# Turning score maxima into rows on VectorE in place of TensorE, in a fused AdaLN block

## The chip, the core and the metric

The kernel runs on one core of one Trainium2 chip. The metric is the device time of one execution in microseconds (us), as a median over several executions. A core has five engines, each with an instruction queue of its own: TensorE (PE, matrix products and transposes, results in PSUM), VectorE (DVE), ScalarE (ACT), GpSimd (POOL) and SyncE (SP, which here only issues DMA transfers).

## The reference, cut to what matters

The reference is one transformer block with adaptive layer norm over x of 4 batches, 1024 tokens and 256 features. Attention has 16 heads of 16 features. Behind it stands a feed-forward stage that chooses one of 8 adapters for each batch.

```python
mod = (silu(c) @ wmod).reshape(4, 6, 1, 256)   # sa, ca, ga, sb, cb, gb; ga and gb kept off zero
h = layernorm(x) * (1 + ca) + sa
q, k, v = split(h @ qkv_w.T)                   # 16 heads of 16
probs = softmax(q @ k.T / 4)                   # 1024 x 1024 per head and batch
x = x + ga * ((probs @ v) @ proj_w.T + proj_b)
h = layernorm(x) * (1 + cb) + sb
# 8 encoder/decoder pairs reconstruct h; the one of least error picks the adapter
x = x + gb * (h @ W_base + b_base + relu(h @ W_down[a] + b_down[a]) @ W_up[a] + b_up[a])
```

The softmax needs the greatest score of each query before it takes exponentials, so that these stay in range.

## The kernel before, in words

**Groups and halves.** Attention is worked in 16 groups: 4 batches times 4 groups of 4 heads. Within a group, the 1024 queries are cut into two halves of 512, and a half into 4 tiles of 128.

**First pass, the maxima (row_max).** For each pair of heads, each query tile and each half of the keys, two matmuls at L607 write scores (ps, 128 queries x 2 heads x 512 keys) to a PSUM buffer of the tag "big". VectorE takes their greatest value along the keys, negated, into mx (L614). A half of a group needs 16 such reductions. Behind the last of them VectorE takes the minimum over the two key halves (L617) and writes it into mpad, a padded 128 x 128 tile. What results has queries along partitions.

**From columns to rows (to_row).** The second pass wants the maxima as rows, queries along the free dimension. One step after the minimum, the transpose is put at the head of a list called urgent. The planner takes it in the middle of the next pair of steps, in place of another dense item. PE turns mpad into pmx (L567), a buffer of the tag "msc", of which there is one; VectorE copies 32 rows of it to SBUF (mfull, L569); GpSimd (for the very first half, where `alone` still holds, VectorE) splits each value into a high part of the shortened type float32r and the rest (mrow, L572 and L573). One step later SP stores the rows of the half to a DRAM scratch tensor (mdram, L576), and one step later again it reads them back into 2 x 4 rows of mt (L587), in the arrangement that the second pass wants. For the very first group (`soon`) store and reading are issued at once.

**Second pass (step_of).** `begin` computes the scores again, turned (pt, keys along partitions, L713): two matmuls of k and q, and two more that add the negated maxima from mt by way of the constant matrices `picks`, high part and rest together. ScalarE takes the exponential (es, L721). `weigh` multiplies es with the values (pv, L667). One step is one tile of 128 keys with one half of the queries; there are 256 steps.

**Buffers that tie the engines together.** ps, pt and the decoder's pr (L834, read by VectorE at L837 into df) share the tag "big", three buffers of two PSUM banks. A fourth such product must wait until the reader of the first, VectorE for ps and pr, ScalarE for pt, has finished.

**Order.** The order of instructions on PE and SP is written out by hand throughout. VectorE, ScalarE and GpSimd follow the hand order in the first group, and after it the order that the framework's scheduler gives. The main loop takes two steps at a time and lays them out by a pattern of letters: t for the two halves of a `begin`, S for score pairs of a later group, V for a `weigh`, R for a decoder product. At the first V it calls `dense`, which takes an item from the streams of pending work (projections, encoders, v and q/k products); `tick` counts down what `defer` has put off. The streams are served by how urgent they are.

**The start.** The first half of group 0 is computed in the opening stage, beside weight transposes and conditioning (the list `beside`). Behind its 16 score products come the transpose, the last `beside` items and two v products (pvp, L466), three more score products, and then the first step.

Of the kernel before, what the change touches and what calls it, by code (L numbers as in the profile page):

```python
# [8 lines left out]
F32 = mybir.dt.float32  # L9
F32R = mybir.dt.float32r  # L10
# [3 lines left out]
ALU = mybir.AluOpType  # L14
# [3 lines left out]
P = 128  # L18
HD = 16
HG = 4  # L20
STRIP = 32
# [5 lines left out]
def tile_adaln_block(  # L27
# [21 lines left out]
    nc = tc.nc  # L49
    B, S, D = x.shape  # L50
    NE, _, FH = w_enc.shape
    R = w_down.shape[2]
    NT = S // P
# [6 lines left out]
    NH = S // HALF  # L60
    TH = HALF // P

    cst = ctx.enter_context(tc.tile_pool(name="cst", bufs=1))
# [14 lines left out]
    st = ctx.enter_context(tc.tile_pool(name="st", bufs=3))  # L78
# [39 lines left out]
    ident = cst.tile([P, P], F32, name="ident")  # L118
# [15 lines left out]
    for n in range(2):  # L134
        t = cst.tile([P, S], F32R, name=f"mt{n}")
# [11 lines left out]
    for n in range(NV):  # L147
        t = cst.tile([P, NT, HG, STRIP], F32, name=f"vaug{n}")
# [31 lines left out]
    mdram = [dram.tile([NH, 2, HG * TH, P], F32, name=f"mdram_{n}") for n in range(2)]  # L180
# [99 lines left out]
    FULL = 0.86  # L280
# [4 lines left out]
    def defer(steps, f):  # L285
        later.append([steps, f])

    def tick():
        for entry in list(later):
            entry[0] -= 1  # L290
            if entry[0] <= 0:
                later.remove(entry)
                entry[1]()

    spare, alone, over = [0], [True], []
# [256 lines left out]


    aT_of = {}
    urgent = []

    def row_max(b, g):

        n = (b * NG + g) % 2
        mx = st.tile([P, NH, NH, HG, TH], F32, tag="mx", name=f"mx_{b}_{g}", bufs=2)  # L560


        soon = b + g == 0

        def to_row(hq):
            pm = msc_tile([P, P], f"pmx_{b}_{g}_{hq}")
            nc.tensor.transpose(pm, mpad[n], ident)  # L567
            mfull = st.tile([HG * NT, P], F32, tag="mfull", name=f"mfull_{b}_{g}", bufs=1)
            nc.vector.tensor_copy(mfull, pm[: HG * NT, :])  # L569
            mrow = st.tile([HG * NT, 2, P], F32R, tag="mrow", name=f"mrow_{b}_{g}", bufs=1)  # L570
            eng = nc.vector if alone else nc.gpsimd
            eng.tensor_copy(mrow[:, 0, :], mfull)  # L572
            eng.tensor_tensor(mrow[:, 1, :], mfull, mrow[:, 0, :].bitcast(F32), ALU.subtract)  # L573

            def store():
                nc.sync.dma_start(  # L576
                    mdram[n][hq].rearrange("l r c -> r l c"),
                    mrow[hq * HG * TH : (hq + 1) * HG * TH].bitcast(F32),
                )
                if soon:  # L580
                    back()
                else:
                    defer(1, back)

            def back():
                for a in range(2):
                    nc.sync.dma_start(  # L587
                        mt[n][a * DUO : a * DUO + HG, hq * HALF : (hq + 1) * HALF].bitcast(F32),
                        mdram[n][hq, :, a * HG * TH // 2 : (a + 1) * HG * TH // 2, :].rearrange(
                            "l (i t) c -> l i (t c)", i=HG // 2  # L590
                        ),
                    )

            if soon:
                store()
            else:
                defer(1, store)

        for half in range(NH):
            pairs = [(i, half, t, h) for h in range(NH) for i in range(2) for t in range(TH)]  # L600
            for i, hq, t, h in pairs:
                q, k = duos["q", b, g, i], duos["k", b, g, i]
                t0 = hq * HALF + t * P
                ps = big_tile([P, 2, HALF], f"ps_{b}_{g}_{hq}_{t}_{h}_{i}")
                for a in range(2):
                    r = slice(a * DUO, (a + 1) * DUO)
                    nc.tensor.matmul(  # L607
                        ps[:, a, :],
                        q[r, t0 : t0 + P],
                        k[r, h * HALF : (h + 1) * HALF],  # L610
                        start=True,
                        stop=True,
                    )
                nc.vector.tensor_reduce(mx[:, h, hq, i::2, t], ps, AX.X, ALU.max, negate=True)  # L614
                if (i, hq, t, h) == pairs[-1]:
                    rows = mpad[n][:, : HG * NT].rearrange("p (q j t) -> p q j t", q=NH, t=TH)
                    nc.vector.tensor_tensor(rows[:, half], mx[:, 0, half], mx[:, 1, half], ALU.min)  # L617
                    defer(1, lambda half=half: urgent.append(("D", 0.0, [lambda: to_row(half)])))
                yield

    def turned(b, ch, h):
# [501 lines left out]
    for i in range(2):  # L1123
        t = cst.tile([P, 1], F32, name=f"row{i}")
# [3 lines left out]
        pick = cst.tile([P, P], F32R, name=f"pick{i}")  # L1128
        nc.vector.tensor_copy(pick, t.to_broadcast([P, P]))
        picks.append(pick)  # L1130
    mpad = []
    for n in range(2):
        t = cst.tile([P, P], F32, name=f"mpad{n}")
        nc.gpsimd.memset(t, 0.0)
        mpad.append(t)
    mean_w = cst.tile([P, P], F32, name="mean_w")
    nc.gpsimd.memset(mean_w, 1.0 / (S * D))
    widened("k", 0, 0)
# [29 lines left out]
    beside += [lambda o=o: turn_weights(wqkv, qn, o, spare_tile) for o in (1, NC + 1)]  # L1168
    beside.append(lambda: turn_biases(spare_tile))
    maxima = row_max(0, 0)  # L1170
    FIRST = PAIRS // NH
    for n in range(FIRST):
# [5 lines left out]
            expand(0, 1, n - 9)  # L1178
        if n and beside:
            beside.pop(0)()  # L1180
    tick()
    all_of(Stream(list(urgent)))
    tick()
    for f in beside + v_first[1:]:
        f()
# [63 lines left out]

    alone.clear()  # L1250
    unweighed = []
    streams = [Stream(urgent)]
    streams[0].at = len(urgent)

    def ready(k, kind):

        found = []
        for s in streams:
            item = s.head(k)
            if item is not None and item[0] == kind:  # L1260
                found.append(s)
        return sorted(found, key=lambda s: (s.head(k)[-1] != "first", -s.pace(k)))

    def take(s, k):
        item = s.head(k)
# [12 lines left out]

    def dense(k, tiles, now):

        moves(k)
        if now and ready(k, "D") and streams[0].head(k) is not None:
            take(streams[0], k)[2][0]()
            return
        small = 2
        while True:
            found = [
                s
                for s in ready(k, "D")
                if s is not streams[0] and (small if s.head(k)[1] < FULL else tiles) > 0  # L1290
            ]
            if not found:
                return
            item = take(found[0], k)
            for f in item[2]:
                f()
            if item[1] < FULL:
                small, tiles = small - 1, tiles if now is False else 0
            else:
                small, tiles = 0, tiles - 1  # L1300
            moves(k)
# [7 lines left out]
    for k0 in range(0, len(order) * NT, 2):  # L1309
        b, g, h = order[k0 // NT]  # L1310
# [17 lines left out]
        tiles = sum(s.head(k0)[1] >= FULL for s in ready(k0, "D"))  # L1328
# [5 lines left out]
        k, n_t, n_s, n_v = k0, 0, 0, 0  # L1334
# [3 lines left out]
        for what in PATTERN[kind]:  # L1338
            if what == "t":
                if n_t % 2 == 0:  # L1340
                    k = k0 + n_t // 2
# [10 lines left out]
            elif what == "V":  # L1352
# [82 lines left out]
```

## Time and profile before

| | |
|---|---|
| median of 3 runs | 1140.88 us (1139.20 to 1141.67) |
| profiled execution, its own time | 1142.01 us |
| its span | 1140.2 us, 16547 instructions |
| granted TensorE clock, mean | 0.987 |
| ScalarE busy | 702.7 us (62%) |
| GpSimd busy | 263.3 us (23%) |
| mx reductions on VectorE, L614 | 512, 614.3 us, 1221 ns each |
| es exponentials on ScalarE, L721 | 512, 509.6 us, 1021 ns each |
| idle time of VectorE in front of L614 | 189.4 us, of it 184.1 us waiting for ps |

The profile page gives the busy time of each engine, then the span cut into 40 slices with the busy share in tenths, then groups of instructions by line with the mean duration. PEld is the weight load of TensorE, which overlaps its matmuls. Ends of matmuls are modelled, so a busy TensorE is not TensorE at its peak, and neighbouring matmuls can overlap in the record. A timeline row gives the start and the busy time in us, the engine, the line, the operation, the tiles it writes and reads, and how many like instructions are merged; a bracket tells of idle time in front of it and of what ended that. In front of a DMA row stands SPq, the queue that issues it, and the time is that of the issue, not of the landing.

### The profile page before, as it was taken

Reading aid. Unit: us, or ns where it says so; the run is one execution under the profiler, and the core shown is the slowest. Engines: PE = TensorE matmul, PEld = TensorE weight load, DVE = VectorE, ACT = ScalarE, POOL = GpSimd, SP = SyncE. Lnnn points to the kernel's source line nnn. Section 1 sums busy time; section 2 is a strip of 40 time slices with the busy share of each in tenths; the row PEclk is TensorE's granted clock in tenths of the full one; section 3 lists DMA queues with packets and bytes.
Section 4 is the critical chain, followed back from the end, with each engine's and each line's share of the span. In section 5 each row is a group of like instructions: output and inputs, shape, how many; then the busy total and the mean of one; then the engine's idle time right before and its main releaser. Section 6 shows DMA issues by size and latency. Waiting matters only on the chain. (4 is left out here: it accounts for less than half of the span.)

```text
span 1140.2 us, 16547 instructions
## 1 busy us (share of the span) xinstructions
PE 1081.3 (95%) x6371; PEld 482.7 (42%) x6371; DVE 803.2 (70%) x969; ACT 702.7 (62%) x953; POOL 263.3 (23%) x310
## 2 busy tenths in 40 slices
PE   8989999999999999999999999999998999899986
PEld 4433434443444444444544443333544334335333
DVE  6677876677777576777678677887688777872454
ACT  3245766666655677776455777776465777754662
POOL 2223234213343130113345000004121000241111
PEclk9899999999999999999999999999999999999998
DMA  5522423231441302122150302020230200101001
GB/s 185 103 66 89 163 81 119 76 132 58 154 136 45 120 17 90 53 95 87 48 183 6 127 13 95 16 91 19 69 130 7 85 15 9 57 23 48 10 0 49
DMA packets 57800, 84.63 MB, mean 74 GB/s; under 512 B 24941, under 2 KB 40325, under 8 KB 55929
## 3 DMA queue, kind: packets, MB, share of 16 engines
q1 hardware_dynamic: 55664, 79.90, 21.6%
q0 software_dynamic: 1088, 2.36, 0.8%
q10 hardware_dynamic: 968, 1.32, 0.3%
q8 instruction: 50, 0.82, 0.3%
q14 instruction: 30, 0.24, 0.1%
HBM read 52.15 MB, written 24.06 MB: 67 GB/s over the span
## 5 line engine op out<-in xcount | busy, mean ns | idle before, releaser
L614 DVE TENSOR_REDUCE mx<-ps 128x2 f32<-128x1024 f32 x512 | 614.3, 1221 | 189.4 <-PE ps L607 184.1
L721 ACT ACTIVATE es<-pt 128x1024 f32<-128x1024 f32 x512 | 509.6, 1021 | 248.2 <-PE pt L713 230.8
L667 PE MATMUL pv<-es,vaug 128*32 128x512 f32 x2048 | 275.1, 608 | 0.5 <-ACT ou L678 0.3
L607 PE MATMUL ps<-k,q 64*128 64x512 f32 x1024 | 237.1, 457 | 16.2 <-DVE mx L614 11.4
L713 PE MATMUL pt<-q,k 64*128 64x512 f32 x1024 | 231.3, 436 | 14.0 <-DVE mx L614 7.1
L713 PE MATMUL pt<-mt,pick 64*128 64x512 f32 x1024 | 209.0, 392 | 0.0
L607 PEld LDWEIGHTS ps<-k,q 64*128 64x128 f32 x1024 | 97.3, 184 | 222.3 <-issue 92.9
L713 PEld LDWEIGHTS pt<-q,k 64*128 64x128 f32 x1024 | 99.8, 185 | 119.8 <-DVE mx L614 87.9
L842 ACT ACTIVATE df<-df,fbias 128x512 f32<-128x512 f32 x128 | 91.1, 713 | 63.0 <-DVE df L837 63.0
L713 PEld LDWEIGHTS pt<-mt,pick 64*128 64x128 f32 x1024 | 100.3, 185 | 12.1
L837 DVE TENSOR_TENSOR df<-pr,h2T 128x1024 f32<-128x1024 f32 x64 | 77.5, 1223 | 22.3 <-PE pr L834 14.3
L667 PEld LDWEIGHTS pv<-es,vaug 128*32 128x32 f32 x2048 | 40.6, 108 | 101.8 <-issue 91.4
L834 PE MATMUL pr<-he,wdec 64*128 64x512 f32 x256 | 65.4, 605 | 3.7 <-ACT es L721 3.2
L572 POOL CAST mrow<-mfull 32x128 fp32r<-32x128 f32 x31 | 8.7, 281 | 252.3 <-DVE mfull L569 244.3
L813 PE MATMUL ph<-h2T,wenc 128*128 128x512 f32 x128 | 64.5, 628 | 0.4 <-ACT h2T L350 0.4
L319 POOL TENSOR_TENSOR rstd_n<-ve_n,neghalf 128x4 f32<-128x4 f32 x16 | 16.5, 1033 | 115.9 <-DVE ve_n L317 113.1
L955 PE MATMUL pf<-wbg,h2T 128*128 128x256 f32 x128 | 36.5, 417 | 0.0
L813 PEld LDWEIGHTS ph<-h2T,wenc 128*128 128x128 f32 x128 | 22.0, 191 | 30.0 <-issue 28.2
L466 PE MATMUL pvp<-wqkv,hT 128*128 128x256 f32 x128 | 34.5, 419 | 0.0
L774 PE MATMUL ppj<-wpg,aT 128*128 128x256 f32 x128 | 31.9, 392 | 1.9 <-ACT he L821 1.9
L975 DVE TENSOR_TENSOR x<-pf,x 128x512 f32<-128x512 f32 x16 | 10.8, 690 | 32.5 <-PE pt L713 20.5
L505 POOL COPY vaug<-vi 128x512 f32<-128x512 f32 x13 | 8.5, 655 | 108.4 <-DMA vi<-vdram 108.4
(153 smaller groups left out, 795.8 us busy)
## 6 DMA issues: line engine op xcount, KB each, us to landing
q<-qdram SPq DMA_DIRECT2D x56, 256.0 KB
k<-kdram SPq DMA_DIRECT2D x56, 256.0 KB
qdram<-qhl SPq DMA_DIRECT2D x7, 1024.0 KB
kdram<-khl SPq DMA_DIRECT2D x7, 1024.0 KB
xin<-in_L_attn_x_dram SPq DMA_DIRECT2D x16, 256.0 KB
vdram<-vo SPq DMA_DIRECT2D x16, 256.0 KB
aT<-ou SPq DMA_DIRECT2D x32, 128.0 KB
x<-in_L_attn_x_dram SPq DMA_DIRECT2D x8, 512.0 KB
```

The source lines that it names most:

```text
L466: nc.tensor.matmul(pv[:, t, :], hT[:, c, t0 : t0 + P], wqkv[:, c, 2 * D : 3 * D], start=(c == 0), stop=(c == NC - 1),)
L607: nc.tensor.matmul(ps[:, a, :], q[r, t0 : t0 + P], k[r, h * HALF : (h + 1) * HALF], start=True, stop=True,)
L614: nc.vector.tensor_reduce(mx[:, h, hq, i::2, t], ps, AX.X, ALU.max, negate=True)
L667: nc.tensor.matmul(acc[h][j * STRIP : (j + 1) * STRIP, :], va[:, kt, j, :], es[j // 2][:, j % 2, :], start=(kt == 0), stop=(kt == NT - 1),)
L713: nc.tensor.matmul(pt[:, a, :], k[r, kt * P : (kt + 1) * P] if first else picks[i][r, :], q[r, hs] if first else mt[n % 2][r, hs], start=f ...
L721: nc.scalar.activation(e, pt, AF.Exp, scale=SCALE)
L774: nc.tensor.matmul(s["po"][:, t, :], aT_of[b, t0 // HALF][:, c, t0 % HALF : t0 % HALF + P], s["wpg"][:, c, :], start=(c == 0), stop=(c == ...
L813: nc.tensor.matmul(s["ph"], wenc[:, c, 2 * pr : 2 * pr + 2, :].rearrange("p n h -> p (n h)"), s["h2T"][:, c, hs], start=(c == 0), stop=(c ...
L834: nc.tensor.matmul(two[:, i, :], wdec[r, pr, c * P : (c + 1) * P], he[r, :], start=True, stop=True)
L837: nc.vector.tensor_tensor(df, two, h2T[:, c, hs].unsqueeze(1).to_broadcast([P, 2, HALF]), ALU.subtract)
L842: nc.scalar.activation(df[:, i, :], df[:, i, :], AF.Square, bias=bdec_of(e, c), accum_out=s["acc"][:, e, c, h : h + 1],)
L955: nc.tensor.matmul(po[u][:, t, :], s["h2T"][:, c, t0 : t0 + P], s["wbg"][:, c, :], start=(c == 0), stop=False,)
```

## The change

The minimum goes to a compact tile (least, 128 x 16). VectorE splits it there into high part and rest (mhl, 128 partitions x 2 x 16), and turns it with its own transpose, which turns each block of 32 x 32 by itself: 128 x 32 becomes four stacked blocks of 32 rows x 32 queries (mrow). Four transfers, one for each block, put the pieces of 128 bytes side by side into mdram. `to_row` is called directly behind the last reduction of a half; store and reading are put off as before. The padded tiles, the transpose on PE, the copy from PSUM, the split on GpSimd, the list urgent and its place in `dense` go.

```diff
+        least = st.tile([P, HG, TH], F32, tag="least16", ...)
 ...
         def to_row(hq):
-            pm = msc_tile([P, P], f"pmx_{b}_{g}_{hq}")
-            nc.tensor.transpose(pm, mpad[n], ident)
-            mfull = st.tile([HG * NT, P], F32, tag="mfull", ...)
-            nc.vector.tensor_copy(mfull, pm[: HG * NT, :])
-            mrow = st.tile([HG * NT, 2, P], F32R, tag="mrow", ...)
-            eng = nc.vector if alone else nc.gpsimd
-            eng.tensor_copy(mrow[:, 0, :], mfull)
-            eng.tensor_tensor(mrow[:, 1, :], mfull, mrow[:, 0, :].bitcast(F32), ALU.subtract)
+            mhl = st.tile([P, 2, HG * TH], F32R, tag="mhl", ..., bufs=2)
+            nc.vector.tensor_tensor(least, mx[:, 0, hq], mx[:, 1, hq], ALU.min)
+            flat = least.rearrange("p j t -> p (j t)")
+            nc.vector.tensor_copy(mhl[:, 0, :], flat)
+            nc.vector.tensor_tensor(mhl[:, 1, :], flat, mhl[:, 0, :].bitcast(F32), ALU.subtract)
+            mrow = st.tile([P, STRIP], F32, tag="mrow", ..., bufs=2)
+            nc.vector.transpose(mrow, mhl.rearrange("p l r -> p (l r)").bitcast(F32))
             def store():
-                nc.sync.dma_start(
-                    mdram[n][hq].rearrange("l r c -> r l c"),
-                    mrow[hq * HG * TH : (hq + 1) * HG * TH].bitcast(F32),
-                )
+                to = mdram[n][hq].rearrange("l r c -> (l r) c")
+                for u in range(P // STRIP):
+                    of = slice(u * STRIP, (u + 1) * STRIP)
+                    nc.sync.dma_start(to[:, of], mrow[of, :])
 ...
                 if (i, hq, t, h) == pairs[-1]:
-                    rows = mpad[n][:, : HG * NT].rearrange("p (q j t) -> p q j t", q=NH, t=TH)
-                    nc.vector.tensor_tensor(rows[:, half], mx[:, 0, half], mx[:, 1, half], ALU.min)
-                    defer(1, lambda half=half: urgent.append(("D", 0.0, [lambda: to_row(half)])))
+                    to_row(half)
 ...
-    all_of(Stream(list(urgent)))
-    tick()
 ...
-        if now and ready(k, "D") and streams[0].head(k) is not None:
-            take(streams[0], k)[2][0]()
-            return
```

More of the change, by code (lines that the diff above doesn't have):

```diff
@@ L554, in tile_adaln_block @@
     aT_of = {}
-    urgent = []
     def row_max(b, g):
@@ L560, in row_max @@
         mx = st.tile([P, NH, NH, HG, TH], F32, tag="mx", name=f"mx_{b}_{g}", bufs=2)
+        least = st.tile([P, HG, TH], F32, tag="least16", name=f"least_{b}_{g}", bufs=2)
         soon = b + g == 0
         def to_row(hq):
-            pm = msc_tile([P, P], f"pmx_{b}_{g}_{hq}")
[L567 to L570, printed above, removed]
-            eng = nc.vector if alone else nc.gpsimd
-            eng.tensor_copy(mrow[:, 0, :], mfull)
-            eng.tensor_tensor(mrow[:, 1, :], mfull, mrow[:, 0, :].bitcast(F32), ALU.subtract)
+            mhl = st.tile([P, 2, HG * TH], F32R, tag="mhl", name=f"mhl_{b}_{g}_{hq}", bufs=2)
+            nc.vector.tensor_tensor(least, mx[:, 0, hq], mx[:, 1, hq], ALU.min)
+            flat = least.rearrange("p j t -> p (j t)")
+            nc.vector.tensor_copy(mhl[:, 0, :], flat)
+            nc.vector.tensor_tensor(mhl[:, 1, :], flat, mhl[:, 0, :].bitcast(F32), ALU.subtract)
+            mrow = st.tile([P, STRIP], F32, tag="mrow", name=f"mrow_{b}_{g}_{hq}", bufs=2)
+            nc.vector.transpose(mrow, mhl.rearrange("p l r -> p (l r)").bitcast(F32))
             def store():
-                nc.sync.dma_start(
-                    mdram[n][hq].rearrange("l r c -> r l c"),
-                    mrow[hq * HG * TH : (hq + 1) * HG * TH].bitcast(F32),
-                )
+                to = mdram[n][hq].rearrange("l r c -> (l r) c")
+                for u in range(P // STRIP):
+                    of = slice(u * STRIP, (u + 1) * STRIP)
+                    nc.sync.dma_start(to[:, of], mrow[of, :])
                 if soon:
@@ L1130, in tile_adaln_block @@
         picks.append(pick)
[L1131 to L1135, printed above, removed]
     mean_w = cst.tile([P, P], F32, name="mean_w")
@@ L1251, in tile_adaln_block @@
     unweighed = []
-    streams = [Stream(urgent)]
-    streams[0].at = len(urgent)
+    streams = []
     def ready(k, kind):
@@ L1289, in dense @@
                 for s in ready(k, "D")
-                if s is not streams[0] and (small if s.head(k)[1] < FULL else tiles) > 0
+                if (small if s.head(k)[1] < FULL else tiles) > 0
             ]
```

## The prediction

> **What bounds the kernel now.** I read the page first: the engine sums, then the slices over time.
>
> ```profile
> PE 1081.3 (95%) x6371; PEld 482.7 (42%) x6371; DVE 803.2 (70%) x969; ACT 702.7 (62%) x953; POOL 263.3 (23%) x310
> ...
> PE   8989999999999999999999999999998999899986
> ...
> DVE  6677876677777576777678677887688777872454
> ```
>
> TensorE (PE) is busy in nearly every slice; VectorE (DVE) stands at 6 to 8 tenths. The table of stages shows how little is left in the middle:
>
> ```profile
> 400.00:600.00 200.00, 198.93 (x1193) 90.56 (x1194) 144.79 (x159) 132.31 (x185) 51.62 (x58) 1.00 0.25 82
> ```
>
> In these 200 us PE rests 1.1 us, at a granted clock of 1.00. So work taken off PE shortens the kernel there, unless another engine makes PE wait instead. The longest waits of the list of waits (244.3 us of POOL for the copy mfull, 275.5 us of the SP queue for mrow) are rests of engines that have nothing else due; taking them away is worth nothing by itself.
>
> Next, the tile that the change abolishes, pmx (columns: count, then least/median/greatest ns):
>
> ```profile
> L567 PE MATMUL pmx<-ident,mpad x32: 328/328/476, 51.7 to 1030.5; 128*128 128x128 f32 x32
> L569 DVE COPY mfull<-pmx x32: 246/278/280, 52.2 to 1030.8; 32x128 f32<-32x128 f32 x32
> ```
>
> **The change part by part.** It happens 32 times: 16 groups of heads, two halves each.
>
> *The transpose on PE.* Its 328 ns overlap the neighbours, so I price it by starts. Timeline of PE around one half (start, us busy):
>
> ```profile
> 514.89 1.06 PE L667 MATMUL pv<-es,vaug 128*32 128x512 f32 x8
> 515.89 0.50 PE L607 MATMUL ps<-k,q 64*128 64x512 f32 x2
> ...
> 520.29 1.06 PE L667 MATMUL pv<-es,vaug 128*32 128x512 f32 x8
> 521.29 0.33 PE L567 MATMUL pmx<-ident,mpad 128*128 128x128 f32 x1
> 521.54 0.51 PE L607 MATMUL ps<-k,q 64*128 64x512 f32 x2
> ```
>
> Without the transpose, ps starts 1.00 us after pv does; with it, 1.25 us. At the trace's full resolution the step is 0.26 us in nearly every half. The first half is counted below; the other 31 give 31 x 0.26 = 8.1 us off PE.
>
> In two of these halves (204.5 and 322.4) PE also rested 1.05 and 0.88 us before the transpose, because its PSUM buffer, the only one of its tag, was still being read by ScalarE (vo). Without the transpose PE goes straight on to ps, and the next user of that buffer comes later. Between nothing and 1.9 us; ScalarE's own es follows closely behind, so I take the middle, 1.0.
>
> *The start.* Here PE has nothing queued before the transpose:
>
> ```profile
> 49.23 0.69 PE L204 MATMUL pw_wqkv<-ident,qn 128*128 128x128 f32 x2
> 51.68 0.45 PE L567 MATMUL pmx<-ident,mpad 128*128 128x128 f32 x1 [1.75 <-DVE mpad L617]
> 52.50 0.29 PE L270 MATMUL pf<-ident,fb 20*128 20x20 f32 x1 [0.37 <-DMA k<-khl]
> 52.72 6.63 PE L466 MATMUL pvp<-wqkv,hT 128*128 128x256 f32 x16
> 59.28 0.96 PE L607 MATMUL ps<-k,q 64*128 64x512 f32 x6
> ...
> 61.56 0.39 PE L713 MATMUL pt<-mt,pick 64*128 64x512 f32 x2
> ```
>
> PE rests 1.75 us for the minimum, turns it, rests 0.37 us for the copy. Afterwards pf can follow pw_wqkv at about 50.1 and all behind it moves up by some 2.4 us, until the first pt needs the rows in mt (61.56, then 59.2). Those rows: the minimum starts at 51.36 on VectorE, and four instructions end about 52.05; four store issues at 0.32 us (the row of this store is 324 ns) end at 53.35. Before, one store ended its issue at 53.37 and its readers mt<-mdram began at 55.31. So the rows come as early as before: reading ends its issue at 56.7, and with the same 1.9 us to land they are there at 58.6, just ahead. I take 2.2 us; were the four landings 1 us later, 1.6 would be left.
>
> Gain together: 8.1 + 1.0 + 2.2 = 11.3 us.
>
> *VectorE.* Removed: the copy from PSUM, 0.28 us a half. Before it VectorE sat idle for PE 17.7 us in all (26 times), which an engine that is not the bottleneck does not get paid for. Added, directly behind the minimum: a cast of 128x16, a subtraction of 128x16, a transpose of 128x32. For the subtraction the nearest row is the minimum itself:
>
> ```profile
> L617 DVE TENSOR_TENSOR mpad<-mx x32: 164/175/1348, 51.4 to 1028.6; 128x16 f32<-128x16 f32 x32
> ```
>
> The cast lies between 0.15 (128x1 casts) and 0.23 (pick, 128x128): 0.155. No transpose is in the trace; 128x32 rows are 0.19 (less_q, a reduction), 0.22 (half, an addition) and 0.35 (a reciprocal): 0.19 as the cheapest plain pass, 0.35 as the upper end. Sum 0.52 us, taken as 0.5, at a place where nothing was before; the copy that goes lay some 6 us later. VectorE's next reduction is queued behind these three, and PE waits for that reduction when it refills the ring of three PSUM buffers. Two places show the difference:
>
> ```profile
> 582.18 0.18 DVE L617 TENSOR_TENSOR mpad<-mx 128x16 f32<-128x16 f32 x1
> 582.81 2.36 DVE L614 TENSOR_REDUCE mx<-ps 128x2 f32<-128x1024 f32 x2 [0.45 <-PE ps L607]
> ```
>
> ```profile
> 735.97 0.17 DVE L617 TENSOR_TENSOR mpad<-mx 128x16 f32<-128x16 f32 x1
> 736.11 1.23 DVE L837 TENSOR_TENSOR df<-pr,h2T 128x1024 f32<-128x1024 f32 x1
> 737.25 2.35 DVE L614 TENSOR_REDUCE mx<-ps 128x2 f32<-128x1024 f32 x2
> ```
>
> In the first, 0.45 us of idle time swallows the burst. In the second VectorE runs without a break, PE refills a buffer as soon as it is free, and the half microsecond reaches PE. Going through the timelines behind the 31 minima, I find 19 halves where idle time of VectorE, or a long dense item of PE, covers it, 7 that pass on all 0.5 us and 5 that pass on 0.17 to 0.28, since PE comes for the buffer later: 7 x 0.5 + 5 x 0.2 = 4.5 us. Bounds: 0 (all hidden) and 31 x 0.5 = 15.5.
>
> The trace holds a warning. Four minima took 0.49, 1.24, 1.32 and 1.35 us, and at 316.0 the long one ends with a GpSimd instruction of 1.28 us (wpg) that started with it. Over 32 that is 0.12 us on average. Two of the new instructions read SBUF in the same way, 0.24 us a half: 12 x 0.24 = 2.9 us in the 12 halves without cover, 31 x 0.24 = 7.4 in all, nothing if they miss GpSimd's work, of which the change leaves less. I take half of the 2.9, 1.5. VectorE's part is then 4.5 + 1.5 = 6.0 us.
>
> The Trainium skill speaks against this part: "VectorE: DVE Perf Modes", section Rules for kernel authors, advises to minimize the number of chained VectorE instructions, since each pays a pipeline flush of its own. By that rule alone, with two instructions more each half, the burst would be all loss and the sum 15.5 - 11.3 = 4.2 us slower; the idle times above say that most of it is covered.
>
> *GpSimd* loses 31 x (0.28 + 0.45) = 22.6 us. It is 23% busy and 0% of the chain that ended last: nothing.
>
> *SP and the transfers.* Each half, one store becomes four: 3 x 32 x 0.32 = 31 us more issue on a queue whose issues sum to some 240 of 1140 us. Store and reads move up by some 5 us, past one or two other issues (vdram<-vo and rdram<-rs at 204.5), which then wait about 1.3 us; the rows are needed much later (in the last group the store goes at 1032.0 and the first pt of that half follows at 1050.7). I cost it at nothing, covered by that lead; without it, a reader of the late transfer would wait up to 1.3 us. The Trainium skill, "DMA: Bandwidth & Descriptors", section Bandwidth, says that transfers below 64 KB are dominated by their descriptors, which speaks against four pieces of 4 KB; no row here has such a store, and by the page it costs latency, which the lead covers everywhere but at the start.
>
> *The freed slot.* The transpose took the place of a dense item in its step; now a pending item may go there. The same items run in all; I cost it at nothing, with 1.1 us either way, the rest that PE had in the whole stage shown above.
>
> **Sum.** 11.3 - 6.0 = 5.3 us. The profiled execution took 1142.0 us (span 1140.2 and 1.8 around it) and would become 1136.7; it lay 1.1 above the median of 1140.9, so I forecast 1135.6.
>
> **The rivals.** *All hidden:* VectorE's idle time between reductions takes the burst everywhere. For it: 189 us of such idle time. Against: the unbroken stretches around 735 and 962. 1140.9 - 11.3 = 1129.6, or 1128.7 with both vo waits.
>
> *No change:* the burst costs an average of 11.3 / 31 = 0.36 us of PE in each half. 1140.9.
>
> *Slower, VectorE's burst becomes the bound:* behind the last reduction of each half, the burst of 0.5 us plus 0.24 of GpSimd interference holds back the ring in every half: 31 x 0.74 = 22.9 against 11.3, 1152.5. It decides from 0.36 us a half on. For it: three buffers only, and PE already waits for mx in many steps; a transpose dearer than 0.35 would do it too. Against: the 19 halves with cover.
>
> **How the numbers follow.** A measurement of this kernel tells about 0.2%, 2.3 us, from no change. Forecast (1132 to 1138.5): 0.41; all hidden: 0.25; no change: 0.14; slower: 0.20. So faster 0.66, same 0.14, slower 0.20. The range goes from 1128.5 (all hidden) to 1143.5, just into the slower case, as far as leaves 2 in 10 out.
>
> **What would show it.** Right: no pmx, pv to ps in 1.00 us at every half; pf behind pw_wqkv without a rest near 50 us, the first pt near 59.3; the three new rows at 0.15 to 0.35 us; longer PE waits for mx or df just behind the minima, some 6 us in sum. Wrong: a transpose row of 0.6 us or more, a first pt that waits for mt, new waits of PE for VectorE in the halves that have cover, or q, k and mt reads that land late because SP stands at the four stores.

## The result, and the profile after

The changed kernel is slower by 0.3%: a median of 1143.80 us (7 runs, 1140.53 to 1144.99) against 1140.33 us of the kernel before beside it (7 runs), a ratio of 1.0029 with a 95% interval from 1.0015 to 1.0042. Measured again (e2 below) it was 1.0019 (1.0006 to 1.0031). The forecast was 1135.6 us, on the other side.

The profiled execution took 1140.53 us, the shortest of the seven; the other six took 1142.8 to 1145.0. So its span, 1138.8 us, is shorter than the 1140.2 of the profile before, and the sign of the result can't be read from the two spans. What can be read from them are the steps. The page of the changed kernel, engine sums, and the stage from 400 to 600 us in the table of stages:

```profile
PE 1073.6 (94%) x6339; PEld 477.1 (42%) x6339; DVE 811.8 (71%) x1031; ACT 702.9 (62%) x953; POOL 240.9 (21%) x246
```

```profile
400.00:600.00 200.00, 198.32 (x1196) 89.77 (x1194) 148.11 (x175) 132.19 (x183) 49.02 (x48) 1.00 0.25 83
```

TensorE has lost 32 instructions and 7.7 us of busy time, but the span only 1.4: its rests have grown by 6.3 us. VectorE is 8.6 us busier, GpSimd 22.4 us less. In the quiet middle PE now rests 1.7 us of 200, where it was 1.1. The costliest groups say where the rests are (behind the bar: idle time just in front of the group, and what ended most of it):

```profile
L607 PE MATMUL ps<-k,q 64*128 64x512 f32 x1024 | 237.1, 457 | 15.2 <-DVE mx L614 10.1
L711 PE MATMUL pt<-q,k 64*128 64x512 f32 x1024 | 231.4, 438 | 19.1 <-DVE mx L614 11.0
...
L832 PE MATMUL pr<-he,wdec 64*128 64x512 f32 x256 | 65.0, 603 | 6.2 <-ACT es L719 3.5
L811 PE MATMUL ph<-h2T,wenc 128*128 128x512 f32 x128 | 65.0, 633 | 4.0 <-ACT h2T L350 4.0
```

The same four groups had 16.2, 14.0, 3.7 and 0.4 us before, 34.3 in all; now they have 44.5. The second and the fourth, before:

```profile
L713 PE MATMUL pt<-q,k 64*128 64x512 f32 x1024 | 231.3, 436 | 14.0 <-DVE mx L614 7.1
L813 PE MATMUL ph<-h2T,wenc 128*128 128x512 f32 x128 | 64.5, 628 | 0.4 <-ACT h2T L350 0.4
```

So 10.2 us of new rests stand in front of the four, and a net 3.9 us went elsewhere (among them the rest for the first minimum and the two waits for vo). The two that grew most point at two different causes: pt waits longer (+5.1, of it 3.9 for VectorE's mx), and ph waits for the turned h2T of the last batch (+3.6), with which the maxima have nothing to do.

The tiles that took the place of pmx and mfull (count, then least/median/greatest ns):

```profile
L568 DVE TENSOR_TENSOR least<-mx x32: 165/176/1044, 52.8 to 1025.0; 128x16 f32<-128x16 f32 x32
L570 DVE CAST mhl<-least x32: 157/174/1232, 53.0 to 1025.2; 128x16 fp32r<-128x16 f32 x32
L571 DVE TENSOR_TENSOR mhl<-least,mhl x32: 174/176/1196, 53.3 to 1025.4; 128x16 fp32r<-128x16 f32 x32
L573 DVE STREAM_TRANSPOSE mrow<-mhl x32: 199/211/214, 53.5 to 1025.6; 128x32 f32<-128x32 f32 x32
```

The medians lie near what was expected (0.17 to 0.21 us). The transpose never takes more than 214 ns; the three in front of it have a tail of over 1 us.

PE around the same half as before, and PE at the start:

```profile
515.25 1.06 PE L665 MATMUL pv<-es,vaug 128*32 128x512 f32 x8
516.24 0.50 PE L607 MATMUL ps<-k,q 64*128 64x512 f32 x2
```

```profile
50.82 0.23 PE L270 MATMUL pf<-ident,fb 20*128 20x20 f32 x1
51.35 3.72 PE L466 MATMUL pvp<-wqkv,hT 128*128 128x256 f32 x16 [0.30 <-ACT wqkv L211]
55.00 0.96 PE L607 MATMUL ps<-k,q 64*128 64x512 f32 x6
57.76 1.12 PE L128 MATMUL warm<-warm 128*128 128x512 f32 x2 [1.79 <-ACT vaug L478]
58.81 0.50 PE L711 MATMUL pt<-q,k 64*128 64x512 f32 x2
59.81 1.09 PE L711 MATMUL pt<-mt,pick 64*128 64x512 f32 x2 [0.50 <-DMA mt<-mdram]
```

The step from pv to ps is 0.99 us: this gain is there. The first pt with mt starts 1.75 us earlier than before (59.81 against 61.56), with mt 0.50 us late, and a new rest of 1.79 us stands in front of warm. But the two starts can't be laid side by side as they are: before, PE ran at half clock from 48.4 to 58.6 us, and the pvp group took 6.63 us there against 3.72 here. Counted from the first minimum to the first pt with mt, it is 10.2 us before (7.3 of them at half clock) and 7.0 here (none); in second profiles it is 8.7 for the kernel before (e1, 3.4 at half clock) and 8.0 for the changed one (e2, 4.4 at half clock). How much the start gained at equal clock stays open.

Now the price. VectorE behind one minimum, where the next reduction's data come late anyhow, and behind another, where nothing is idle:

```profile
577.10 0.17 DVE L568 TENSOR_TENSOR least<-mx 128x16 f32<-128x16 f32 x1
577.31 0.17 DVE L570 CAST mhl<-least 128x16 fp32r<-128x16 f32 x1
577.52 0.17 DVE L571 TENSOR_TENSOR mhl<-least,mhl 128x16 fp32r<-128x16 f32 x1
577.73 0.21 DVE L573 STREAM_TRANSPOSE mrow<-mhl 128x32 f32<-128x32 f32 x1
577.87 2.31 DVE L614 TENSOR_REDUCE mx<-ps 128x2 f32<-128x1024 f32 x2
```

```profile
730.79 0.18 DVE L568 TENSOR_TENSOR least<-mx 128x16 f32<-128x16 f32 x1
...
731.56 1.18 DVE L835 TENSOR_TENSOR df<-pr,h2T 128x1024 f32<-128x1024 f32 x1
```

Each of the four reads what the one in front of it wrote, and they start 0.21 us apart though each is busy for 0.17. In the second place df starts 0.77 us behind the minimum; before it was 0.14. So the burst adds 0.63 us where it isn't covered, not 0.5.

And the burst behind which PE rests longest, all engines, cut to the rows that matter; below it PE at the same place in the profile before:

```profile
984.89 4.98 POOL L765 TENSOR_TENSOR x<-x,gpb 128x512 f32<-128x512 f32 x4 [14.21 <-DMA x<-in_L_attn_x_dram]
...
987.62 1.04 DVE L568 TENSOR_TENSOR least<-mx 128x16 f32<-128x16 f32 x1
...
988.70 1.20 DVE L570 CAST mhl<-least 128x16 fp32r<-128x16 f32 x1
...
990.28 1.18 DVE L835 TENSOR_TENSOR df<-pr,h2T 128x1024 f32<-128x1024 f32 x1
...
991.52 0.51 PE L711 MATMUL pt<-q,k 64*128 64x512 f32 x2 [1.94 <-DVE df L835]
```

```profile
994.44 0.51 PE L713 MATMUL pt<-q,k 64*128 64x512 f32 x2 [0.57 <-DVE df L837]
```

While GpSimd works through four additions of some 1.24 us, the minimum and the cast behind it take over 1 us each, and PE rests 1.94 us where it was 0.57. In all, 9 of the 96 instructions (least, cast, subtraction) took over 0.4 us, and each of the nine ends 29 to 34 ns behind the end of a GpSimd instruction that had started before it.

### The profile page after: what moved, and what is told of

Its sections match the earlier page's. It is cut to its first block, busy times and chain, and to the rows that moved or that the text cites. A ratio compares the mean times of both kernels' runs of the same rounds, so it can differ in the third digit from the quotient of the medians.

```text
span 1138.8 us, 16558 instructions
## 1 busy us (share of the span) xinstructions
PE 1073.6 (94%) x6339; PEld 477.1 (42%) x6339; DVE 811.8 (71%) x1031; ACT 702.9 (62%) x953; POOL 240.9 (21%) x246
## 4 chain that ended last, share of the span: by engine, by line
PE 71%; DVE 15%; ACT 5%; DMA 4%; issue 2%; SPq 1%; POOL 1%; POOLq 0%; DVEq 0%; ACTq 0%
PE pv L665 19%; PE pt L711 17%; PE ps L607 12%; DVE mx L614 8%; PE ph L811 5%; PE pr L832 3%; DVE df L835 3%; ACT es L719 2%; PE pvp L466 2%; PE ppj L772 2%; PE pq L432 2%; PE pf L953 2%; PE pk L432 2%; DMA k<-kdram 1%; PE ptn_n L347 1%
## 5 line engine op out<-in xcount | busy, mean ns | idle before, releaser
L643 POOL TENSOR_TENSOR aT<-aT,su 128x512 f32<-128x512 f32 x14 | 18.0, 1283 | 204.0 <-DMA su<-rdram 156.4
L832 PEld LDWEIGHTS pr<-he,wdec 64*128 64x128 f32 x256 | 23.3, 187 | 26.1 <-issue 9.5
L819 ACT ACTIVATE he<-ph,fbias 128x512 f32<-128x512 f32 x32 | 21.9, 686 | 19.1 <-PE ph L811 19.1
L466 PE MATMUL pvp<-wqkv,hT 128*128 128x256 f32 x128 | 31.6, 391 | 0.3 <-ACT wqkv L211 0.3
```

Source lines behind the costliest of these rows:

```text
L466: nc.tensor.matmul(pv[:, t, :], hT[:, c, t0 : t0 + P], wqkv[:, c, 2 * D : 3 * D], start=(c == 0), stop=(c == NC - 1),)
L832: nc.tensor.matmul(two[:, i, :], wdec[r, pr, c * P : (c + 1) * P], he[r, :], start=True, stop=True)
```

## The experiments

Three theories were set against each other. BURST: the three added VectorE instructions cost more than the 6.0 us of the forecast. ORDER: the place in `dense` that the transpose had taken is now open to other items, the order changes, and late in the kernel that costs. START: something in the opening stage, the rest in front of warm above all, or its effect on the clock. Ratios are to the kernel before, run beside it on the same chip, with 95% intervals.

| run | median us | ratio |
|---|---|---|
| e1, kernel before again | 1141.36 | 0.9991 (0.9975 to 1.0006) |
| e2, changed kernel again | 1143.73 | 1.0019 (1.0006 to 1.0031) |
| e3, two vo buffers | 1143.96 | 1.0024 (1.0009 to 1.0039) |
| e4, before without the transpose | 1131.24 | 0.9904 (0.9886 to 0.9923) |
| e5, turned first, split on GpSimd | 1136.89 | 0.9969 (0.9957 to 0.9982) |
| e6, burst twice | 1145.36 | 1.0036 (1.0022 to 1.0049) |
| e7, place held empty | 1140.19 | 0.9996 (0.9983 to 1.0010) |
| e8, first half by TensorE | 1143.89 | 1.0031 (1.0020 to 1.0042) |
| e9, e5 and e7 together | 1132.78 | 0.9945 (0.9927 to 0.9963) |
| e10, e4 with the place open | 1133.43 | 0.9945 (0.9932 to 0.9958) |
| e11, one store | 1141.00 | 1.0011 (1.0000 to 1.0022) |
| e12, before with the burst added | 1148.00 | 1.0081 (1.0065 to 1.0097) |

**The two kernels again (e1, e2).** No edit.

> The kernel before, unchanged, run for the granted clock of each execution. Three theories are compared in all runs. START: the start of the changed kernel (VectorE's chain, four stores and two reads in front of the v stores on SP, ScalarE waiting for its one vo buffer) leaves TensorE short of work, so that in most executions the clock gate grants half speed for longer; BURST: three extra VectorE instructions behind each minimum hold back the PSUM ring; ORDER: the freed dense slot packs pending products differently. START expects 1140 us at a mean clock near 0.987 in most executions, against 0.979 to 0.984 of the changed kernel. BURST and ORDER expect the same mean clock in both kernels, near 0.982.

> The changed kernel, unchanged, for a second profile and more clocks. START: about 1143.8 us, and a profile whose mean clock is near 0.982 shows some 10 us more of half speed than the first profile of this kernel (31.8 us), most of it between 45 and 75 us. BURST: half speed as in the first profile, and the time between 300 and 1000 us longer by 3 us than there.

The kernel before agrees with itself. The changed kernel is again slower, and its granted clock is lower in the median: 0.9845 against 0.988. Over the runs of one kernel, a clock lower by 0.001 goes with some 0.7 us, so 0.0035 is about 2.5 us, as much as the whole difference; straight lines through the runs of both give 1142.1 and 1142.5 us at a clock of 0.987. So the loss goes with a lower clock; which part of the edit lowers it, the later runs tell. The profile of e2 (1148.60 us) shows the other end of the spread: 51 us of its span at half speed, against 30 us in the first profile of the same kernel.

**The start (e3, e8).** e3 takes the rest in front of warm away, by a second buffer for vo:

```diff
-tag="vo", ..., bufs=1
+tag="vo", ..., bufs=2
```

> The changed kernel with two vo buffers in place of one: ScalarE needs not wait for the store of the last v product at 51 to 57 us. START: about 3 us faster than the changed kernel, 1140 to 1141 us, TensorE's rest of 1.8 us before the warm product gone, mean clock 0.985 or more. BURST: 1143 to 1144, no change. ORDER: no change.

1.0024: no change. Timeline of PE at the start of e3:

```profile
56.10 1.12 PE L128 MATMUL warm<-warm 128*128 128x512 f32 x2
57.15 0.51 PE L711 MATMUL pt<-q,k 64*128 64x512 f32 x2
60.77 0.76 PE L711 MATMUL pt<-mt,pick 64*128 64x512 f32 x2 [3.11 <-DMA mt<-mdram]
```

warm follows without a rest, pt starts 1.7 us earlier, and PE then stands 3.11 us for mt. The rest has only moved to the next thing that is late, the rows.

e8 gives the very first half back to TensorE, with its copy from PSUM and its one store; the other 31 stay turned on VectorE.

```diff
+            if soon and hq == 0:
+                by_tensor()     # mpad, pmx, mfull, split, one store, as before
+                return
```

> The changed kernel with the first half of the first group alone turned as before, on TensorE with one store of 16 KB. START: the rows reach mt some 0.7 us earlier and TensorE does not outrun them; 2 to 3 us faster than the changed kernel, 1141 to 1142, mean clock near 0.987. BURST: 1143 to 1144 at a clock of 0.984. ORDER: no change.

1.0031: the loss is all there without the new start, so START falls as a cause. What the start had gained doesn't show in the time either.

**The gain by itself (e4).** The kernel before without the transpose on PE and the copy from PSUM; GpSimd splits the untransposed mpad, so the maxima are wrong and the rest of the work stays.

```diff
-            pm = msc_tile([P, P], ...)
-            nc.tensor.transpose(pm, mpad[n], ident)
-            mfull = st.tile([HG * NT, P], F32, tag="mfull", ...)
-            nc.vector.tensor_copy(mfull, pm[: HG * NT, :])
+            mfull = mpad[n][: HG * NT, :]
```

> The kernel before with the transpose on TensorE and the copy of its result from PSUM left out; GpSimd splits rows of the unturned tile, so the numbers in the maxima are wrong. This is the gain of the change alone, nothing added on VectorE. The prediction's sum: 11.3 us less, 1129. If the 0.26 us per half were not on the path: less than 4 us, 1136.5 or more. START allows for anything between, since the start moves too: 1130 to 1135.

0.9904 is 11.0 us (8.8 to 13.0), where the prediction summed 11.3. The sum of the gain was right; the loss lies in what is paid for it, some 13 to 14 us where 6 were counted. Not all of the 11.0 are the rests and steps that were priced: the median clock rose from 0.988 to 0.991, by the 0.7 us above an estimated 2 us, and the two rests for vo are gone but a rest of 1.99 us at 288.8 is new.

**The burst (e12, e6, e5).** e12 adds the cast, the subtraction and the transpose behind each minimum of the kernel before, into tiles that nothing reads; PE's transpose and all else stay.

```diff
                     nc.vector.tensor_tensor(rows[:, half], mx[:, 0, half], mx[:, 1, half], ALU.min)
+                    nc.vector.tensor_copy(mhl[:, 0, :], flat)
+                    nc.vector.tensor_tensor(mhl[:, 1, :], flat, mhl[:, 0, :].bitcast(F32), ALU.subtract)
+                    nc.vector.transpose(turned_rows, mhl.rearrange("p l r -> p (l r)").bitcast(F32))
```

> The kernel before with the three VectorE instructions added behind each minimum, into tiles that nobody reads; transpose, copy, slot and transfers stay as they were. This is the cost of the burst alone. The prediction's 6.0 us: 1.0053 of the kernel before. BURST as the trace of the changed kernel has it (0.63 us from the minimum's start on, 12 halves without cover, and rests that draw the clock down): 7 to 9 us, 1.006 to 1.008. If the burst were harmless and ORDER all of the loss: 1.000 to 1.002.

1.0081 is 9.2 us (7.4 to 11.1). Its trace, laid beside that of before half by half, has 9.9 us more over halves 2 to 31. Of these, 3.0 come in two places where the clock fell to half for 3.4 us (786.0 and 1018.1), each behind a rest of 1.21 us. The kernel before has these rests as well, at full clock in its first profile; in its second (e1) the rest at 1008.9 is followed by half clock too. The other 6.9 are spread over the halves: an estimated 2 in the four halves where GpSimd holds the burst up (314.0, 545.2, 797.9, 996.7) and 5 in the others. In the median the clock of e12 is that of the kernel before beside it, 0.989.

e6 doubles the burst in the changed kernel: a second cast, subtraction and transpose into tiles of their own.

```diff
             nc.vector.transpose(mrow, mhl.rearrange("p l r -> p (l r)").bitcast(F32))
+            nc.vector.tensor_copy(mhl2[:, 0, :], flat)
+            nc.vector.tensor_tensor(mhl2[:, 1, :], flat, mhl2[:, 0, :].bitcast(F32), ALU.subtract)
+            nc.vector.transpose(mrow2, mhl2.rearrange("p l r -> p (l r)").bitcast(F32))
```

> The changed kernel with cast, subtraction and transpose done a second time into tiles that nobody reads: 0.56 us more on VectorE behind each minimum. BURST: the idle times of 0.45 us are used up, so most halves pass it on: 31 x 0.4 = 12 us slower than the changed kernel, 1153 to 1157. START: only the first half counts, 1144 to 1145. ORDER: no change.

A miss: 1145.36, not 10 us more. VectorE's timeline in e6 says why:

```profile
734.23 0.18 DVE L568 TENSOR_TENSOR least<-mx 128x16 f32<-128x16 f32 x1
734.44 0.18 DVE L570 CAST mhl<-least 128x16 fp32r<-128x16 f32 x1
734.53 0.17 DVE L576 CAST mhl<-least 128x16 fp32r<-128x16 f32 x1
734.65 0.18 DVE L571 TENSOR_TENSOR mhl<-least,mhl 128x16 fp32r<-128x16 f32 x1
734.75 0.17 DVE L577 TENSOR_TENSOR mhl<-least,mhl 128x16 fp32r<-128x16 f32 x1
734.90 0.21 DVE L573 STREAM_TRANSPOSE mrow<-mhl 128x32 f32<-128x32 f32 x1
735.04 0.17 DVE L579 STREAM_TRANSPOSE mrow<-mhl 128x32 f32<-128x32 f32 x1
735.13 1.18 DVE L841 TENSOR_TENSOR df<-pr,h2T 128x1024 f32<-128x1024 f32 x1
```

The scheduler laid the second chain into the gaps of the first: an instruction that does not need the one in front of it starts 0.09 to 0.14 us behind it, and each starts 0.21 us or more behind the one that it needs. From the minimum to df it is 0.90 us with seven instructions, against 0.77 with four. The experiment did not double the cost it was to double, and says nothing on how much of it reaches PE. What it does show is that on VectorE the burst takes its time by the chain of dependences more than by the count.

e5 shortens the burst: the minimum goes into a 128 x 32 tile, VectorE turns that at once, and GpSimd splits the rows; the four stores carry 16 rows x 2.

```diff
-            nc.vector.tensor_copy(mhl[:, 0, :], flat)
-            nc.vector.tensor_tensor(mhl[:, 1, :], flat, mhl[:, 0, :].bitcast(F32), ALU.subtract)
-            nc.vector.transpose(mrow, ...)
+            nc.vector.transpose(mturn, least)          # least: 128 x 32, the right half zero
+            eng = nc.vector if alone else nc.gpsimd
+            eng.tensor_copy(mrow[:, 0, :], mturn)
+            eng.tensor_tensor(mrow[:, 1, :], mturn, mrow[:, 0, :].bitcast(F32), ALU.subtract)
```

> The changed kernel with the order of its steps turned round: VectorE takes the minimum into a 128x32 tile of which 16 columns count, transposes that, and GpSimd splits the rows (VectorE in the first half of all). Behind the minimum VectorE then has one instruction (about 0.21 us) in place of three (0.56 us), and none of the two that stood 1.2 us behind GpSimd. BURST: 4 to 6 us faster than the changed kernel, 1138 to 1139.5, mean clock near 0.987. START: no change, since the first half is as long as before, 1143 to 1144. ORDER: no change.

0.9969, that is 5.7 to 6.8 us less than the two ratios of the changed kernel. Its tiles:

```profile
L571 DVE STREAM_TRANSPOSE mturn<-wide x32: 195/211/213, 51.7 to 1019.0; 128x32 f32<-128x32 f32 x32
L574 POOL CAST mrow<-mturn x31: 199/209/217, 84.7 to 1019.3; 128x32 fp32r<-128x32 f32 x31
L575 POOL TENSOR_TENSOR mrow<-mturn,mrow x31: 250/253/254, 85.0 to 1019.6; 128x32 fp32r<-128x32 f32 x31
```

None of these rows has a tail. The shorter chain and the absence of a cast and a subtraction on VectorE that collide with GpSimd give back most of what the burst cost; this run does not part the two. The clock did not rise to the 0.987 that was expected, its median stays at 0.9845.

**The place in the order (e7, e10).** e7 is the changed kernel, with the place that the transpose had in its step kept empty:

```diff
                     to_row(half)
+                    defer(1, lambda: urgent.append(0))
 ...
+        if now and urgent:
+            urgent.pop()
+            return
```

> The changed kernel with the dense slot that the transpose took kept empty, so that products come in the order of the kernel before. ORDER: 2 to 3 us faster, 1141 to 1142. BURST and START: within 1 us of the changed kernel.

0.9996: 2.6 to 3.8 us less than the changed kernel, by an edit that adds nothing but an empty place. e10 does the reverse on e4, with the same wrong maxima: the place is open, so a dense item follows the urgent one in the same step.

```diff
         if now and ready(k, "D") and streams[0].head(k) is not None:
             take(streams[0], k)[2][0]()
-            return
```

> The kernel before without the transpose on TensorE and its copy (wrong maxima), and now also without the held slot: a pending product follows in the same step. Against the same kernel with the slot held (0.9904 of the kernel before). ORDER: 2 to 3 us slower, 0.9925 to 0.9935, a longer rest of TensorE in the closing stage, mean clock 0.987 in place of 0.991. BURST alone: 0.9904, no change.

0.9945 against 0.9904 of e4: 4.7 us, give or take about 2.6, lost, more than the 2 to 3 expected. The closing stage, behind the last pt, as a row of the table of stages, first e4, then e10 (start and end, length, busy us of PE, PEld, DVE, ACT, POOL, granted clock):

```profile
1057.30:1129.70 72.40, 56.15 (x200) 25.63 (x196) 36.35 (x65) 32.89 (x79) 8.83 (x8) 0.93 0.08 23
```

```profile
1056.60:1130.60 74.00, 55.59 (x196) 26.54 (x192) 36.44 (x65) 32.56 (x78) 8.82 (x8) 0.87 0.08 23
```

With the place open, PE has four products fewer left for this stage (encoder products of some 0.5 us each, which went ahead of the last pt), and yet the stage takes 1.6 us longer, at a clock of 0.87 instead of 0.93. The timelines name the new rest, e10 and then e4:

```profile
1082.86 0.72 ACT L839 ACTIVATE df<-df,fbias 128x512 f32<-128x512 f32 x1 [1.94 <-DVE df L834]
...
1085.69 1.42 ACT L350 ACTIVATE h2T<-ptn_n,modc 128x512 f32<-128x512 f32 x2
...
1086.50 3.78 PE L810 MATMUL ph<-h2T,wenc 128*128 128x512 f32 x4 [3.99 <-ACT h2T L350]
```

```profile
1084.14 1.45 ACT L350 ACTIVATE h2T<-ptn_n,modc 128x512 f32<-128x512 f32 x2 [1.20 <-PE ptn_n L347]
...
1084.97 3.60 PE L810 MATMUL ph<-h2T,wenc 128*128 128x512 f32 x4 [0.43 <-ACT h2T L350]
```

The last encoder products need h2T, which ScalarE writes from the turned layer norm of the last batch (ptn_n). In e4 ScalarE has nothing else to do and starts on h2T as soon as ptn_n comes. In e10 twelve decoder products stand in front of ptn_n where eight did; when ptn_n is there, ScalarE first works through four df instructions of these (1082.86 to 1085.79), and PE stands 3.99 us. So the freed place reaches PE by way of another engine's order.

This is no peculiarity of one trace. In all eight profiles with the place open (the changed kernel twice, e3, e5, e6, e8, e10, e11) the four df instructions stand in front of h2T, PE waits 3.99 us there, and its rests behind the last pt sum to 13.2 or 13.3 us; in the six with it held (before, e1, e4, e7, e9, e12) none stands there, PE waits 0.43 us or not at all, and the sum is 9.9 to 10.5. At half clock this stage spends 15.8 to 21.7 us in the first kind and 8.2 to 13.3 in the second; it lasts 73.2 us on average against 71.6, with four products fewer. That this is all of the 4.7 us is not shown: the spans of the two profiles, e4 and e10, differ by only 0.8 us.

**The four stores (e11).** One store in place of four, which sends the first block's rows to all four places, so that the maxima are wrong.

```diff
-                for u in range(P // STRIP):
-                    of = slice(u * STRIP, (u + 1) * STRIP)
-                    nc.sync.dma_start(to[:, of], mrow[of, :])
+                nc.sync.dma_start(
+                    to.rearrange("r (u c) -> r u c", u=P // STRIP),
+                    mrow[:STRIP, :].unsqueeze(1).to_broadcast([STRIP, P // STRIP, STRIP]),
+                )
```

> The changed kernel with one store in place of four: it writes the first block's rows four times, so three quarters of the maxima are wrong. The descriptors stay, three issues of each half go from SP. If the four issues matter anywhere: 1 us or more faster than the changed kernel, and the first rows reach mt 1.5 us earlier. BURST and ORDER: 1.002 to 1.003 of the kernel before, no change.

1.0011, 0.9 to 2.1 us less than the changed kernel, with intervals that overlap. Whether the four issues cost 1 or 2 us or nothing stays open.

**Together (e9).** The edits of e5 and e7 in one kernel.

> Transpose first and split on GpSimd, with the dense slot kept empty as in the kernel before. If BURST and ORDER are two separate terms, they add: 3 us under the first of these alone, 0.9940 of the kernel before (1134 us where that takes 1140.5), mean clock 0.987 or more. If the held slot gained its 3 us only by giving VectorE time behind the burst, so that both are one term: 0.9965, no better than transpose first alone.

0.9945, 6.3 us faster than the kernel before, and 2.7 us faster than e5 alone: within the noise the two terms add. This version beats both kernels.

## Why the prediction was wrong

**The sum, with measured terms.** Predicted: 11.3 gained, 6.0 lost to the burst, the place in the order at nothing: 5.3 us faster. Measured, each part in a kernel of its own: 11.0 gained (e4), 9.2 lost to the burst (e12), 4.7 lost to the open place (e10 against e4): 2.9 us slower. The whole change measured 2.2 (1.0019) and 3.3 us (1.0029). So the parts account for the result, within intervals of about 2 us each. (e4 drops out of this sum: e10 alone is 6.3 us faster, and the burst takes 9.2.)

**The gain: right in sum, in part by luck.** The step from pv to ps is 0.99 us as forecast. The start's 2.2 us are not confirmed: they were read from a profile that ran at half clock there, and e8, which gives the start back, leaves the time where it was (1.0031). In the forecast of mt, "just ahead", the minimum came 1.5 us later than assumed (52.83, not 51.36), and the four issues took 0.49 us each instead of 0.32. The middle value for vo, 1.0, met a new rest of 1.99 us in e4. What filled the sum up to 11.0 is in part the clock, which it did not have.

**VectorE's burst: mechanism right, mis-sized.** "Sum 0.52 us, taken as 0.5" added up busy times. What holds the next reduction back is the distance of starts, 0.21 us along a chain of dependent instructions, 0.63 us added where df follows. With that, 7 x 0.63 + 5 x 0.25 would have been 5.7 us instead of 4.5, and the bound for all halves 19.5 instead of 15.5. The transpose, taken at 0.19 us with 0.35 as the upper end, was 0.211. The collisions with GpSimd were forecast at up to 7.4 us on VectorE, 1.5 of them passed on; the casts and subtractions that took over 0.4 us come to some 6.7 us above their medians. But they come in heaps, two or three in one burst (at 540, 790 and 988), and a delay of 2 us passes any cover that would hide half a microsecond. In all, e12 puts the term at 9.2 us (7.4 to 11.1) where 6.0 was forecast. In its trace 6.9 of 9.9 are left without the two places at half clock, an estimated 5 outside the collisions (4.5 forecast) and 2 in them (1.5); whether the 3.0 at half clock belong to the burst is open. The rule that was weighed against this part, fewer chained instructions, would have given 4.2 us slower, nearer than the sum that was chosen, but by luck: it took the burst for all loss, and many halves cover it (577.10).

**The freed place: the term put at nothing.** This is the step that failed. "I cost it at nothing, with 1.1 us either way" rested on the rest of PE in the stage from 400 to 600 us. There it is still about right, 1.7 against 1.1 us. The cost lies in the last 70 us, which the prediction did not look at: "The same items run in all" holds, but in another order, and ScalarE then has four df instructions in front of the h2T that PE waits for. Measured three ways: 4.7 us (e10 against e4), 2.6 to 3.8 (e7 against the changed kernel), 2.7 (e9 against e5). With the place held, the changed kernel measures no change (e7, 0.9996), which was the forecast's 0.14 case: the mis-sized burst used up the gain, the open place made it a loss.

**GpSimd, SP.** GpSimd's 22.4 us of relief were put at nothing; no run has them alone, and the parts above add up without them. SP's issues took 0.42 us in the median where 0.32 was taken; e11 points to 2 us or less for them, and does not settle it.

**The rivals.** "Slower" named the burst as the bound in every half and the sign as turning from 0.36 us a half on; e12 gives 9.2 / 31 = 0.30, since in many halves it is covered (577.10). The result came out on its side, at a quarter of its price, by a second term that none of the rivals had.

**The clock.** Nothing in the prediction spoke of it. In every pair that differs in the place alone, the kernel with the place open has the lower median clock: 0.9845 for the changed one (e2) against 0.987 (e7), 0.9845 (e5) against 0.991 (e9), 0.987 (e10) against 0.991 (e4). The burst alone leaves it where it was (e12, 0.989). So the clock's part of the loss goes with the open place, whose closing stage spends more time at half clock, and not with the start, to which the text of e1 gave it (e8, without the new start, 0.984). In all traces the stretches at half clock last 3.4 us or a multiple (3.4, 6.8, 10.2), the last one of a run cut off. The Trainium skill, "TensorE: Matmul & The Clock Gate", Part 1: The HAM clock gate, tells of a window of about 3.4 us that runs freely, and of half rate after an idle one; the length agrees. Its section Why this matters for your kernels warns of gaps of over about 3 us. Here all 14 profiles have a rest of 1.20 to 1.22 us in front of pt at the same two places of their work (774 to 786 us and 999 to 1018 us), and in 5 of the 28 cases half clock begins within some 0.5 us behind it; so a shorter rest can be followed by it, and what decides is not shown.

**The tail of the small instructions.** The minimum, the cast and the subtraction took up to 1.23 us beside GpSimd and then ended with its instruction; the transpose never took more than 214 ns, in 32 instances here and 32 each in e5 and e9, though 15 of these 96 ran while a GpSimd instruction was under way. The Trainium skill, "SBUF — State Buffer", section SBUF: two separate sides, says that VectorE and GpSimd share a pair of ports under an exclusive lock, which concerns VectorE's instructions with two SBUF inputs or in a two-port mode, and that the loser waits for the whole instruction. The nine long rows look like that; no run here tests the lock itself.

## What to carry to other kernels

Work that is taken off the bounding engine opens a place in its order, and what slips into that place shifts what follows, on other engines too: look at the end of the kernel, where PE waits for a late result with little left to do beside it, before that is costed at nothing, and try the edit with the place held empty. Count a chain of small dependent instructions by the distance of their starts, not by their busy time, and turn first and split afterwards on an engine that has room. Look at the clock before two stretches are compared: one at half clock makes a gain look larger than it is. A difference of a few tenths of a per cent can't be read from one profile each: the changed kernel's first profile was shorter than that of before, and the median was longer.

## What the runs showed of the hardware that was not expected

- Dependent VectorE instructions of 0.17 us busy start 0.21 us apart; independent ones, laid between them in e6, 0.09 to 0.14 us. Seven instructions took 0.90 us where four took 0.77.
- VectorE's transpose of 128 x 32 f32 took 195 to 214 ns in the changed kernel, e5 and e9, with GpSimd busy or not; the 128 x 16 minima, casts and subtractions beside it took up to 1.23 us in the changed kernel, and the nine long ones ended 29 to 34 ns behind a GpSimd instruction.
- The same rest of 1.2 us was followed by 3.4 us at half clock in 5 of 28 cases. Two profiles of the same kernel spent 30 and 51 us of their spans at half clock, 8 us of time apart.
